# The filter's first layer and its linear part as bfloat16 passes over features split in three stacked parts, from the 61st supertile on, in a graph-convolution kernel

## The chip, the cores and the metric

The kernel runs on one core of a Trainium2 chip. The metric is the device time of one execution in microseconds (us); less is better. Before the change it is 4114.15 us, the median of three runs (4108.7, 4114.15 and 4114.17).

## The reference

A graph layer with N = 12500 nodes, E = 400000 edges sorted by target node (`dst`, the operand that picks rows of h), 128 features and 20 edge attributes:

```python
h = relu(layernorm(x)) @ W_in2f.T                       # 12500 x 128
Wij = smu(f_ij @ W_f1.T + b_f1) @ W_f2.T + b_f2         # the filter, 400000 x 128
x_ij = h[idx_j] * (Wij * rcut_ij[:, None])              # idx_j = dst, sorted
agg = segment_sum(x_ij, idx_i)                          # idx_i = src, in no order
out = x + smu(agg @ W_o1.T + b_o1) @ W_o2.T + b_o2
# smu(z) = ((1 + a) z + (1 - a) z erf(mu (1 - a) z)) / 2, a = 0.01, mu = 2.5
```

`smu` is a scaled GELU plus a small linear part (`LIN`), so the filter is a product with W_f1, a bend, and a product with W_f2. All is float32.

## The kernel before

Edges are handled in tiles of 128, groups of four tiles (512 edges, `GRP`) and supertiles of two groups (1024 edges, `SUP`): 3125 tiles, 782 groups, 391 supertiles. The supertiles are cut into nine epochs (`PARTS`: 59, 59, 59, 59, 48, 37, 27, 27, 16). In an epoch, each tile's 128 messages are scattered into a DRAM buffer with a region for each bin of 128 target rows; in the next epoch that buffer is read back and summed, while the new messages go to the next buffer, and the buffer after that is cleared.

The order on TensorE (PE), VectorE (DVE), ScalarE (ACT) and SyncE (SP) is the order of the code, written by hand; each of these engines works through its queue in that order. One turn of the loop over groups (from L888) does for group g, in software-pipelined order:

- `load(s + 3)` (L431, every second group; SP): the 20 rows of features `f_t` of a supertile (L438) into one of four float32 buffers `fbufs`, whose row 20 holds ones for the bias; then `targets` (L443, the row `rbc` broadcast to 128 partitions, L448) and `window` (L455, two transfers `hw` of 42 rows of h in three bfloat16 parts, L462).
- clearing (L178) of the next buffer, and in `fetch` (L672, L679) reading of the last one, both on SP.
- `turn(g)` (L629): four PE products with w_o1 per group into `pt`; `send(g)` (L638): ACT scales them by the edge weight into `ms` (L642, L645; six buffers of one group each), and GpSimd (POOL) issues four indirect scatters (L648), one per tile.
- `weigh(g + 1)` (L609, L615): the float32 product of w_f2 with the bent layer; `gather` (L596) a bfloat16 one-hot product; `take` (L604) its copy on ACT; `mix` (L620, L625) on DVE.
- `hide(g + 2)` (L555, L562): the float32 product of w_f1 with the features, into `pu`; `bend` (L565, L570): GELU on ACT; `smooth` (L573, L578): `sm = LIN * pu + ge` on DVE, one 128x512 pass.
- `bins`, `count`, `read`, `number`, `pick` (L477 to L551 and L465, L471): places in the buffers, on DVE and PE; `parts`/`add` (L724, L694, L703): the sums of the last epoch's buffer on PE, with `choose` (L690) and the addition to `agg` (L716) on DVE.

In the first epoch, `step` (L877) spreads the setup over the turns: the rows of h (`rows_of_h`, L200 to L230, which split a float32 tile in three bfloat16 parts by `tensor_sub`, L222 and L226) and the index tables. After the last group the last buffer is summed and the output layer is run (L944 to L1022).

Of the kernel before, what the change touches and what calls it, by code (L numbers as in the profile page):

```python
# [19 lines left out]
P = 128  # L20
# [6 lines left out]
LIN = ALPHA / GC  # L27

SUP = 8
GRP = 4  # L30
# [3 lines left out]
ROW = P + 1  # L34
# [6 lines left out]
def gnn_kernel(  # L41
# [19 lines left out]
    nc = tc.nc  # L61
    N, D = x.shape
    R, E = f_t.shape
# [4 lines left out]
    def chunks(total, step):  # L68
        return [(a, min(step, total - a)) for a in range(0, total, step)]
# [28 lines left out]
    const = ctx.enter_context(tc.tile_pool(name="const", bufs=1))  # L98
# [4 lines left out]
    bufs = [dram.tile([NB * CAP[k], ROW], F32, name=f"buf{k}") for k in range(EPOCHS)]  # L103
# [3 lines left out]
    ident = const.tile([P, P], F32, name="ident")  # L107
# [19 lines left out]
    lift = const.tile([P, P], F32, name="lift")  # L127
# [8 lines left out]
    onesb = const.tile([P, P], F32, name="onesb")  # L136
# [2 lines left out]
    NC = (NT + CH - 1) // CH  # L139
    bad = const.tile([P, 4 + 2 * EPOCHS], F32, name="bad")  # L140
    lh = const.tile([P, 2, NC], F32, name="lh")
    b1w = const.tile([P, P], F32, name="b1w")
    nc.vector.memset(bad, 0.0)


# [6 lines left out]
    w_in = const.tile([P, P], F32, name="w_in")  # L152
    w_f1 = const.tile([P, P], F32, name="w_f1")
    w_f2 = const.tile([P, P], F32, name="w_f2")
    b2 = const.tile([P, 1], F32, name="b2")
    b2row = const.tile([1, P], F32, name="b2row")
    b1 = const.tile([P, 1], F32, name="b1")
    bz = const.tile([P, 1], F32, name="bz")
    w_o1 = const.tile([P, P], F32, name="w_o1")
    w_o2 = const.tile([P, P], F32, name="w_o2")  # L160
# [113 lines left out]
    with tc.tile_pool(name="ld", bufs=4) as ld, \  # L274
# [8 lines left out]
        irow_ps = ps1.tile([P, GRP * P], F32, name="irow_ps")[:, 0:P]  # L283
        nc.vector.tensor_copy(irow_ps, irow)

        NF = 4
        fbufs = [ld.tile([P, SUP * P], F32, name=f"f{i}", bufs=1) for i in range(NF)]

        def fill(i, engine):
            engine.memset(fbufs[i], 1.0)  # L290

        FEW = 6 * SUP

        def parts_tile():
            return edge.tile([P, GRP, 3, D], BF, name="hs")

        early = (eps_of[0][1] + 3) * PER

        def bank(name):
            return ps2.tile([P, GRP, P], F32, name="pg")  # L300
# [105 lines left out]
        zr = edge.tile([P, 3 * D], BF, name="zr", bufs=1)  # L406
        nc.gpsimd.memset(zr, 0.0)
        nc.gpsimd.dma_start(h_dram[NB * P:N + P, :], zr[:N + P - NB * P, :])
        fill(3, nc.gpsimd)
        nc.gpsimd.memset(x_sb[:, NB - 1, :], 0.0)  # L410
        spare = const.tile([P, 2], F32, name="spare")
        nc.scalar.activation(spare[:, 0:1], eps, AF.Sqrt)
# [16 lines left out]
        loaded, onehot, bins_of, slots, hidden, taken = {}, {}, {}, {}, {}, {}  # L429

        def load(s):  # L431
            if s >= NS:
                return
            t0, nt = sups[s]
            e0, n = t0 * P, nt * P
            fb = fbufs[s % NF]
            if s > 0:
                nc.sync.dma_start(fb[0:R, :n], f_t[:, e0:e0 + n])  # L438
            loaded[s] = (fb,)
            if s > 2:  # L440
                targets(s)

        def targets(s):  # L443

            t0, nt = sups[s]
            e0, n = t0 * P, nt * P
            rb = ld.tile([P, SUP * P], BF, name="rbc")
            nc.sync.dma_start(rb[:, :n], rel_dram[:, e0:e0 + n].to_broadcast([P, n]))  # L448
            loaded[s] += (rb,)
            if s < FEW // SUP:  # L450
                loaded[s] += (h_first.rearrange("p b k d -> p (b k d)"),)
            else:
                window(s)
# [99 lines left out]
        units_of = {}  # L553

        def hide(g):  # L555

            if g >= NG:
                return
            n = groups[g][1] * P
            o = g % PER * GRP * P  # L560
            pu = ps1.tile([P, GRP * P], F32, name="pu")
            nc.tensor.matmul(pu[:, :n], w_f1, loaded[g // PER][0][:, o:o + n], start=True, stop=True)  # L562
            units_of[g] = pu

        def bend(g):  # L565
# [7 lines left out]
        def smooth(g):  # L573
            if g >= NG:
                return
            n = groups[g][1] * P
            sm = edge.tile([P, GRP * P], F32, name="sm")
            nc.vector.scalar_tensor_tensor(sm[:, :n], units_of.pop(g)[:, :n], LIN, hidden[g][:, :n],  # L578
                                           op0=ALU.mult, op1=ALU.add)
            hidden[g] = sm  # L580

        rows_of = {}

# [25 lines left out]
        def weigh(g):  # L609

            if g >= NG:
                return
            n = groups[g][1] * P
            pw = ps1.tile([P, GRP * P], F32, name="pw")
            nc.tensor.matmul(pw[:, :n], w_f2, hidden.pop(g)[:, :n], start=True, stop=True)  # L615
            pws[g] = pw

        mixed = {}
# [169 lines left out]
        pb1 = spread_group(1)  # L788
# [28 lines left out]
        def output_bias():  # L817

            nc.vector.tensor_scalar(w_o2, w_o2, GC, None, op0=ALU.mult)
            nc.vector.tensor_scalar(bz, b1, ZS, None, op0=ALU.mult)  # L820
            nc.vector.tensor_scalar(b1w, onesb, b1, LIN, op0=ALU.mult, op1=ALU.mult)
            pb1 = bank("pb1")[:, 0, :]
            nc.tensor.matmul(pb1, b1w, w_o2, start=True, stop=True)
            nc.vector.tensor_add(bo2, bo2, pb1)

        def named(make, names):

# [23 lines left out]
        steps = [one["placed"], loads.pop(0), one["limits"]]  # L851
# [18 lines left out]
        for i in range(0, len(units_of_rows), 2):  # L870
            for pair in zip(*units_of_rows[i:i + 2]):
                steps += pair
        steps.append(output_bias)
        COUNT = len(steps)
        taken_steps = slot = 0

# [11 lines left out]
        for g in range(NG):  # L888
            s = g // PER
            k = epoch[s]  # L890
            g0, ng = eps_of[k][0] * PER, min(eps_of[k][1] * PER, NG - eps_of[k][0] * PER)
            i = g - g0
            if g == (FEW // SUP - 3) * PER:
                assert not opening
            if g % PER == 0:
                load(s + 3)
            if i == 0:
                cleared = 0
            if g < BY:

                while at_first < min(len(cleans) - 1, -(-(g - 5) * (len(cleans) - 1) // (BY - 12))):
                    apart(clear(0, at_first, nc.sync), "filled", "cleared")
                    at_first += 1
            elif k + 1 < EPOCHS:
                past = BY if k == 0 else 0
                upto = min(len(cleans), -(-(i + 1 - past) * len(cleans) // (ng - 4 - past)))
                while cleared < upto:
                    clear(k + 1, cleared, nc.sync)
                    cleared += 1
            if k and i == 0:  # L910
                work = [(b, q) for b in range(NB) for q in range(Q[k - 1])]
                done = 0
            if k and i == 1:
                begin(k - 1)
            if k and i == WAIT - 2:
                choose(k - 1, 0)
            lo = hi = 0
            if k and i >= WAIT:
                upto = len(work) - (LEFT if k == EPOCHS - 1 else 0)
                lo = upto * (i - WAIT) // (ng - WAIT)  # L920
                hi = upto * (i + 1 - WAIT) // (ng - WAIT)
            if g:
                turn(g)
                send(g)
            step()
            number(g + 1)
            weigh(g + 1)
            gather(g + 1)
            take(g + 1)
            parts(k - 1, lo + (hi - lo) // 2)  # L930
            mix(g + 1)
            step()
            hide(g + 2)
            bend(g + 2)
            count(g + 2)
            smooth(g + 2)
            if g % PER == 0:
                pick((g + 4) // PER)
            bins(g + 3)
            read(g + 2)  # L940
            parts(k - 1, hi)
            step()
            assert k == 0 or taken_steps == COUNT
        k = EPOCHS - 1  # L944
# [32 lines left out]

        def between():
            unit, ge = opened.pop(0)
            sm = edge.tile([P, GRP * P], F32, name="sm")  # L980
            nc.gpsimd.tensor_add(sm[:, :width(unit)], part_of(unit), ge[:, :width(unit)])
            smoothed.append((unit, sm))

# [55 lines left out]
    with tc.If(flag > 0):  # L1039
        with tc.tile_pool(name="gl", bufs=1) as gl, tc.tile_pool(name="gps", bufs=1, space=PSUM) as gps:  # L1040
# [9 lines left out]
            fb = gl.tile([R + 1, P], F32, name="gfb")  # L1050
            nc.vector.memset(fb, 1.0)
            with tc.For_i(0, NT, 1) as t:
# [119 lines left out]
```

## Time and profile before

| what | value |
|---|---|
| median of three runs | 4114.15 us |
| the profiled execution | 4108.47 us |
| its span, first to last instruction | 4106.6 us |
| PE / DVE / ACT / POOL busy | 3668.0 / 3445.1 / 1948.2 / 3081.7 us |
| scatters on POOL (L648) | 3125, mean 964 ns |
| `smooth` on DVE (L578) | 782, mean 685 ns |
| moved by DMA | 820.83 MB, mean 200 GB/s |
| granted TensorE clock | 0.978 |

The profile is of one execution. The span is the time between its first and last instruction; the remaining 1.9 us of that execution lie around it. [...] The DMA share is the mean busy share of 16 DMA engines. A matmul of float32 is recorded as two passes, one of bfloat16 as one.

### The profile page before, as it was taken

The numbers are of one execution on the slowest core, as the hardware profiler recorded it, in microseconds if no ns is written. First come the engines' busy times: TensorE is split into PE (matmuls) and PEld (weight loads), VectorE is DVE, ScalarE is ACT, GpSimd is POOL, SyncE is SP. The second block draws the span as 40 slices with busy tenths as digits, with TensorE's granted clock in tenths as the row PEclk, the third lists the DMA queues.
The fourth block names the chain that finished last, engine by engine and source line by source line (L and its number), as shares of the span: only waits on it lengthen the run. The fifth ranks groups of instructions, "written<-read, shape, count | busy, mean of one in ns | idle before, by whom it ended". The sixth has DMA issues, their size and how long they took to land.

```text
span 4106.6 us, 74086 instructions
## 1 busy us (share of the span) xinstructions
PE 3668.0 (89%) x21117; PEld 2553.0 (62%) x21117; DVE 3445.1 (84%) x7657; ACT 1948.2 (47%) x5690; POOL 3081.7 (75%) x3199
## 2 busy tenths in 40 slices
PE   7878887998979998979998979999899989999897
PEld 4445545666656666646666656666677667666677
DVE  8898887888868888868888868888899889988896
ACT  4557764544444444434544434444444444444441
POOL 6777777777777777777777777777777777777775
PEclk9999999999999999999999989999999999999999
DMA  6976656776647676757667747777689699887568
GB/s 188 232 189 179 195 166 198 204 201 197 195 130 220 204 204 186 201 152 206 202 197 198 198 147 204 208 204 212 179 229 223 186 244 242 221 228 217 164 194 250
DMA packets 564246, 820.83 MB, mean 200 GB/s; under 512 B 178033, under 2 KB 378488, under 8 KB 563698
## 3 DMA queue, kind: packets, MB, share of 16 engines
q1 hardware_dynamic: 449760, 601.83, 54.7%
q0 software_dynamic: 100320, 207.40, 15.9%
q10 hardware_dynamic: 13746, 6.80, 0.6%
q8 instruction: 167, 2.74, 0.3%
q14 instruction: 253, 2.07, 0.2%
HBM read 442.34 MB, written 373.37 MB: 199 GB/s over the span
## 4 chain that ended last, share of the span: by engine, by line
PE 38%; DVE 28%; DMA 19%; ACT 6%; issue 5%; POOL 2%; DVEq 0%; SPq 0%; ACTq 0%; POOLq 0%
DMA buf<-ms,ix 17%; PE pt L635 11%; PE pg L703 8%; DVE se L690 8%; PE pw L615 8%; PE pu L562 7%; DVE mt L625 5%; DVE so L496 4%; DVE sm L578 3%; DVE sl L540 3%; ACT ms L645 2%; ACT ge L570 2%; POOL buf L648 2%; PE ph L596 2%; DVE agg L716 1%
## 5 line engine op out<-in xcount | busy, mean ns | idle before, releaser
L648 POOL DMA_INDIRECT buf<-ms,ix x3125 | 3011.3, 964 | 981.5 <-issue 384.1
L645 ACT ACTIVATE ms<-pt,w_sb 128x128 f32<-128x128 f32 x3125 | 889.0, 368 | 1122.7 <-PE pt L635 1115.4
L635 PE MATMUL pt<-w_o,mt 128*128 128x128 f32 x6250 | 883.7, 285 | 386.0 <-DVE mt L625 382.4
L703 PEld LDWEIGHTS pg<-se,rw 128*128 128x128 f32 x8036 | 1052.5, 192 | 246.5 <-issue 209.7
L703 PE MATMUL pg<-se,rw 128*128 128x128 f32 x8036 | 1149.1, 280 | 2.9 <-DVE se L690 2.9
L635 PEld LDWEIGHTS pt<-w_o,mt 128*128 128x128 f32 x6250 | 768.5, 194 | 472.9 <-DVE mt L625 468.9
L496 DVE SCALAR_TENSOR_TENSOR so<-irow_ps,hi_f,so 128x98 f16<-128x98 f32 x3116 | 989.5, 318 | 82.6
L615 PE MATMUL pw<-sm,w_f 128*128 128x512 f32 x1564 | 823.0, 609 | 10.7 <-DVE sm L578 8.8
L562 PE MATMUL pu<-f,w_f 128*128 128x512 f32 x1564 | 807.3, 598 | 0.0
L625 DVE SCALAR_TENSOR_TENSOR mt<-pw,b,hg 128x512 f32<-128x512 f32 x782 | 583.9, 747 | 201.3 <-ACT hg L604 198.0
L570 ACT ACTIVATE ge<-pu 128x512 f32<-128x512 f32 x782 | 468.4, 599 | 533.2 <-PE pu L562 524.6
L578 DVE SCALAR_TENSOR_TENSOR sm<-pu,ge 128x512 f32<-128x512 f32 x782 | 535.8, 685 | 185.6 <-ACT ge L570 179.2
L690 DVE TENSOR_TENSOR se<-irow_ps,rw 128x1536 f32<-128x1536 f32 (+1 forms) x345 | 588.0, 1704 | 114.0 <-DMA rw<-buf 109.1
L604 ACT ACTIVATE hg<-ph 128x512 f32<-128x512 f32 x782 | 468.5, 599 | 59.7 <-PE ph L596 42.9
L540 DVE TENSOR_REDUCE sl<-pc 128x4 f32<-128x392 f32 x782 | 434.7, 556 | 0.0
L642 ACT ACTIVATE ms<-lo_b 128x4 f32<-128x4 bf16 x782 | 160.1, 205 | 339.8 <-DMA buf<-ms,ix 339.4
L596 PE MATMUL ph<-oh,hw 126*128 126x512 bf16 x770 | 297.0, 386 | 0.0
L562 PEld LDWEIGHTS pu<-f,w_f 128*128 128x128 f32 x1564 | 251.9, 195 | 52.2 <-issue 40.9
L510 PE MATMUL pc<-so,tri 128*128 128x392 f16 x782 | 257.8, 330 | 0.4 <-DVE so L496 0.2
L615 PEld LDWEIGHTS pw<-sm,w_f 128*128 128x128 f32 x1564 | 241.3, 195 | 23.6 <-DVE sm L578 20.2
L512 PEld LDWEIGHTS <-rest_h 128*128 128x128 f16 x781 | 76.3, 98 | 263.1 <-issue 263.1
L512 PE MATMUL pc<-so,rest_h 128*128 128x294 f16 x781 | 225.5, 289 | 0.0
(153 smaller groups left out, 1386.9 us busy)
## 6 DMA issues: line engine op xcount, KB each, us to landing
rw<-buf SPq DMA_DIRECT2D x292, 774.0 KB
rbc<-rel_dram SPq DMA_DIRECT2D x389, 256.0 KB
buf<-zero SPq DMA_DIRECT2D x243, 387.0 KB
buf<-ms,ix POOLq DMA_INDIRECT x3125
buf<-zero SPq DMA_DIRECT2D x193, 258.0 KB
rw<-buf SPq DMA_DIRECT2D x49, 645.0 KB
f<-in_f_t SPq DMA_DIRECT2D x390, 80.0 KB
hw<-h_dram SPq DMA_DIRECT2D x770, 31.5 KB
```

The lines of the kernel that those rows point to most:

```text
L496: nc.vector.scalar_tensor_tensor(so[:, j], irow_ps[:, :NB], hi_f[:, t + j:t + j + 1], so[:, j - 1] if j else before, op0=ALU.is_equal, op1 ...
L540: nc.vector.tensor_reduce(sl[:, :n], pc[:, :n], op=ALU.max, axis=AX.X)
L562: nc.tensor.matmul(pu[:, :n], w_f1, loaded[g // PER][0][:, o:o + n], start=True, stop=True)
L570: nc.scalar.activation(ge[:, :n], units_of[g][:, :n], AF.Gelu, scale=ZS)
L578: nc.vector.scalar_tensor_tensor(sm[:, :n], units_of.pop(g)[:, :n], LIN, hidden[g][:, :n], op0=ALU.mult, op1=ALU.add)
L615: nc.tensor.matmul(pw[:, :n], w_f2, hidden.pop(g)[:, :n], start=True, stop=True)
L625: nc.vector.scalar_tensor_tensor(mt[:, :n], pws.pop(g)[:, :n], b2, rows_of.pop(g)[:, :n], op0=ALU.add, op1=ALU.mult)
L635: nc.tensor.matmul(pt[:, j, :], mt[:, j * P:(j + 1) * P], w_o1, start=True, stop=True)
L645: nc.scalar.activation(ms[:, j, 0:P], pt[:, j], AF.Copy, scale=w_sb[:, t + j:t + j + 1])
L648: i = nc.gpsimd.indirect_dma_start(out=bufs[k][:, :], out_offset=bass.IndirectOffsetOnAxis(ap=ix[:, j:j + 1], axis=0), in_=ms[:, j, :], in ...
L690: nc.vector.tensor_tensor(se[:, :m], irow_ps.unsqueeze(1).to_broadcast([P, m, P]), rows_in[c][:, :m, P:P + 1].to_broadcast([P, m, P]), op= ...
L703: nc.tensor.matmul(pgs[0][:, g, :], rows_in[c][:, o, 0:P], sel[c][:, o, :], start=(q == 0), stop=(q == Q[k] - 1))
```

## The change

From supertile 60 on (`PLAIN`), the features of a supertile stand as three bfloat16 parts that add up to the float32 value, stacked in one tile: 60 rows of the first part three times, 40 rows of the second twice, 20 rows of the third, and three rows of ones (123 rows). The weights W_f1 stand in three parts opposite to them (`ws_f`), so that one bfloat16 pass over 123 rows gives the product. The linear part `LIN * (W_f1 f + b) W_f2` is a second bfloat16 pass (`ws_c`) that opens the accumulation of `pw`; `smooth` does nothing there. The features come in chunks of six supertiles (`SEG`): one load into `fx` (120 rows), four ACT copies and four DVE subtractions split them, one of these eight in each turn (`splits`), and three SBUF-to-SBUF transfers per supertile stack them (`load`). Six new steps at the end of the first epoch make the weights. `rbc` has three buffers where it had four, `fbufs` three (each of two halves) where it had four; the output layer's `sm` uses the `ms` buffers.

```diff
+        NF = 3
+        HALVES = 2
+        SEG = P // R
+        PLAIN = eps_of[0][1] + 1
+        fx = ld.tile([P, SUP * P], F32, name="fx", bufs=1)
         def fill(i, engine):
             engine.memset(fbufs[i], 1.0)
+            engine.memset(fbufs[i][96:P, :].bitcast(BF), 1.0)
...
-        fill(3, nc.gpsimd)
...
-            if s > 0:
+            if s >= PLAIN:
+                fb = stack_of(s)
+                c, j = (s - PLAIN) // SEG, (s - PLAIN) % SEG
+                a = 0
+                for q in range(3):
+                    r = 3 - q
+                    nc.sync.dma_start(fb[a:a + r * R, :n],
+                                      parts_of[c][j * R:(j + 1) * R, q, :n].unsqueeze(1).to_broadcast([R, r, n]))
+                    a += r * R
+            elif s > 0:
                 nc.sync.dma_start(fb[0:R, :n], f_t[:, e0:e0 + n])
...
+        def split(c, i):
...
+            if i < 0:
+                if whole:
+                    nc.sync.dma_start(fx[0:whole * R, :],
+                                      f_t[:, e0:e0 + whole * SUP * P].rearrange("k (s e) -> s k e", e=SUP * P))
...
+            part = parts_of[c]
+            kind, half = i // 2, i % 2
+            o = half * (SUP * P // 2)
...
+            f32, of = fx[:rows, o:o + w], lambda q: part[:rows, q, o:o + w]
+            if kind == 0:
+                nc.scalar.activation(of(0), f32, AF.Copy)
+            elif kind == 1:
+                nc.vector.tensor_sub(f32, f32, of(0))
+            elif kind == 2:
+                nc.scalar.activation(of(1), f32, AF.Copy)
+            else:
+                nc.vector.tensor_sub(of(2), f32, of(1))
+        def splits(g):
+            c, i = divmod(g - PER * (PLAIN - 3 - SEG) - 4, PER * SEG)
+            if c >= 0 and i < 8:
+                split(c, i)
+            if c >= -1 and i == 8:
+                split(c + 1, -1)
...
-            rb = ld.tile([P, SUP * P], BF, name="rbc")
+            rb = ld.tile([P, SUP * P], BF, name="rbc", bufs=3)
...
-            nc.tensor.matmul(pu[:, :n], w_f1, loaded[g // PER][0][:, o:o + n], start=True, stop=True)
+            w = w_f1 if g // PER < PLAIN else ws_f
+            nc.tensor.matmul(pu[:, :n], w, loaded[g // PER][0][:, o:o + n], start=True, stop=True)
...
-            sm = edge.tile([P, GRP * P], F32, name="sm")
-            nc.vector.scalar_tensor_tensor(sm[:, :n], units_of.pop(g)[:, :n], LIN, hidden[g][:, :n],
-                                           op0=ALU.mult, op1=ALU.add)
-            hidden[g] = sm
+            pu, ge = units_of.pop(g), hidden[g]
+            if g // PER < PLAIN:
+                nc.vector.scalar_tensor_tensor(ge[:, :n], pu[:, :n], LIN, ge[:, :n], op0=ALU.mult, op1=ALU.add)
...
-            nc.tensor.matmul(pw[:, :n], w_f2, hidden.pop(g)[:, :n], start=True, stop=True)
+            folded = g // PER >= PLAIN
+            if folded:
+                nc.tensor.matmul(pw[:, :n], ws_c, loaded[g // PER][0][:, o:o + n], start=True, stop=False)
+            nc.tensor.matmul(pw[:, :n], w_f2, hidden.pop(g)[:, :n], start=not folded, stop=True)
...
+        def crossed():
+            nc.gpsimd.memset(ws_f, 0.0)
+            nc.gpsimd.memset(ws_c, 0.0)
...
+        weight_steps = [crossed, combined, lambda: cut_weights(w_f1, pieces()[0]), lambda: cut_weights(lift, pieces()[1]),
+                        stacked, restored]
...
             smooth(g + 2)
+            splits(g)
...
-            sm = edge.tile([P, GRP * P], F32, name="sm")
+            sm = msg.tile([P, GRP, ROW], F32, name="ms").rearrange("p b r -> p (b r)")[:, :GRP * P]
```

More of the change, by code (lines that the diff above doesn't have):

```diff
@@ L141, in gnn_kernel @@
     lh = const.tile([P, 2, NC], F32, name="lh")
-    b1w = const.tile([P, P], F32, name="b1w")
     nc.vector.memset(bad, 0.0)
@@ L154, in gnn_kernel @@
     w_f2 = const.tile([P, P], F32, name="w_f2")
+    ws_f = const.tile([P, P], BF, name="ws_f")
+    ws_c = const.tile([P, P], BF, name="ws_c")
     b2 = const.tile([P, 1], F32, name="b2")
@@ L284, in gnn_kernel, with stack_of @@
         nc.vector.tensor_copy(irow_ps, irow)
-        NF = 4
+        NF = 3
+        HALVES = 2
+        SEG = P // R
+        assert SEG >= 6 and 6 * R + 3 <= P
+        PLAIN = eps_of[0][1] + 1
         fbufs = [ld.tile([P, SUP * P], F32, name=f"f{i}", bufs=1) for i in range(NF)]
+        fx = ld.tile([P, SUP * P], F32, name="fx", bufs=1)
         def fill(i, engine):
             engine.memset(fbufs[i], 1.0)
+            engine.memset(fbufs[i][96:P, :].bitcast(BF), 1.0)
+        def stack_of(s):
+            half = s // NF % HALVES
+            return fbufs[s % NF].bitcast(BF)[:, half * SUP * P:(half + 1) * SUP * P]
         FEW = 6 * SUP
         def parts_tile():
-            return edge.tile([P, GRP, 3, D], BF, name="hs")
+            whole = edge.tile([P, 3, SUP * P], BF, name="hs").rearrange("p q e -> p (q e)")
+            return whole[:, :GRP * 3 * D].rearrange("p (n k d) -> p n k d", k=3, d=D)
         early = (eps_of[0][1] + 3) * PER
@@ L441, in load, with chunk_of @@
                 targets(s)
+        parts_of = {}
+        def chunk_of(c):
+            s0 = PLAIN + c * SEG
+            return s0, min(SEG, NS - s0)
+        def split(c, i):
+            s0, m = chunk_of(c)
+            if m <= 0:
+                return
+            e0, whole = sups[s0][0] * P, sum(sups[s0 + j][1] == SUP for j in range(m))
+            rows = m * R
+            cols = sups[s0][1] * P if m == 1 else SUP * P
+            if i < 0:
+                if whole:
+                    nc.sync.dma_start(fx[0:whole * R, :],
+                                      f_t[:, e0:e0 + whole * SUP * P].rearrange("k (s e) -> s k e", e=SUP * P))
+                for j in range(whole, m):
+                    n = sups[s0 + j][1] * P
+                    e = sups[s0 + j][0] * P
+                    nc.sync.dma_start(fx[j * R:(j + 1) * R, :n], f_t[:, e:e + n])
+                return
+            if i == 0:
+                parts_of[c] = edge.tile([P, 3, SUP * P], BF, name="hs")
+            part = parts_of[c]
+            kind, half = i // 2, i % 2
+            o = half * (SUP * P // 2)
+            w = min(cols, o + SUP * P // 2) - o
+            if w <= 0:
+                return
+            f32, of = fx[:rows, o:o + w], lambda q: part[:rows, q, o:o + w]
[13 more added lines that the diff above has]
+                split(c + 1, -1)
         def targets(s):
@@ L614, in weigh @@
             pw = ps1.tile([P, GRP * P], F32, name="pw")
-            nc.tensor.matmul(pw[:, :n], w_f2, hidden.pop(g)[:, :n], start=True, stop=True)
+            o = g % PER * GRP * P
+            folded = g // PER >= PLAIN
+            if folded:
+                nc.tensor.matmul(pw[:, :n], ws_c, loaded[g // PER][0][:, o:o + n], start=True, stop=False)
+            nc.tensor.matmul(pw[:, :n], w_f2, hidden.pop(g)[:, :n], start=not folded, stop=True)
             pws[g] = pw
@@ L820, in output_bias, with pieces, combined, cut_weights @@
             nc.vector.tensor_scalar(bz, b1, ZS, None, op0=ALU.mult)
-            nc.vector.tensor_scalar(b1w, onesb, b1, LIN, op0=ALU.mult, op1=ALU.mult)
+            nc.vector.tensor_scalar(lift, onesb, b1, LIN, op0=ALU.mult, op1=ALU.mult)
             pb1 = bank("pb1")[:, 0, :]
-            nc.tensor.matmul(pb1, b1w, w_o2, start=True, stop=True)
+            nc.tensor.matmul(pb1, lift, w_o2, start=True, stop=True)
             nc.vector.tensor_add(bo2, bo2, pb1)
+        kept = [None]
+        def pieces():
+            return kept[0][:, :, 0:P], kept[0][:, :, P:2 * P]
+        def crossed():
+            nc.gpsimd.memset(ws_f, 0.0)
+            nc.gpsimd.memset(ws_c, 0.0)
+            kept[0] = edge.tile([P, 3, SUP * P], BF, name="hs")
+            pb = bank("pb1")[:, 0, :]
+            nc.tensor.transpose(pb, w_f1, ident)
+            nc.scalar.activation(lift, pb, AF.Copy)
+        def combined():
+            pb = bank("pb1")[:, 0, :]
+            nc.tensor.matmul(pb, lift, w_f2, start=True, stop=True)
+            nc.vector.tensor_scalar(lift, pb, LIN, None, op0=ALU.mult)
+        def cut_weights(w, to):
+            nc.scalar.activation(to[:, 0], w, AF.Copy)
+            nc.vector.tensor_sub(onesb, w, to[:, 0])
+            nc.scalar.activation(to[:, 1], onesb, AF.Copy)
+            nc.vector.tensor_sub(to[:, 2], onesb, to[:, 1])
+        def stacked():
+            for w, to in zip((ws_f, ws_c), pieces()):
+                a = 0
+                for q in range(3):
+                    r = 3 - q
+                    nc.sync.dma_start(w[a:a + r * R, :], to[0:R, 0:r, :])
+                    a += r * R
+                for q in range(3):
+                    nc.sync.dma_start(w[a + q:a + q + 1, :], to[R:R + 1, q, :])
+        def restored():
+            nc.vector.memset(onesb, 1.0)
+        weight_steps = [crossed, combined, lambda: cut_weights(w_f1, pieces()[0]), lambda: cut_weights(lift, pieces()[1]),
+                        stacked, restored]
         def named(make, names):
@@ L873, in gnn_kernel @@
         steps.append(output_bias)
+        steps += weight_steps
         COUNT = len(steps)
```

## The prediction, made before the changed kernel was run

> **What bounds the kernel now.** First the page's busy times, its chain of waits and its costliest group:
>
> ```profile
> PE 3668.0 (89%) x21117; PEld 2553.0 (62%) x21117; DVE 3445.1 (84%) x7657; ACT 1948.2 (47%) x5690; POOL 3081.7 (75%) x3199
> ...
> PE 38%; DVE 28%; DMA 19%; ACT 6%; issue 5%; POOL 2%; DVEq 0%; SPq 0%; ACTq 0%; POOLq 0%
> ...
> L648 POOL DMA_INDIRECT buf<-ms,ix x3125 | 3011.3, 964 | 981.5 <-issue 384.1
> ```
>
> These name PE and DVE, the engines that the change relieves. The third line speaks against them: POOL's 3125 scatters last 964 ns and have 981.5 us of idle before them, 0.31 us each. Is that waiting, or the price of issuing a scatter? The busy times in equal stretches of 500 us tell (columns: PE, PEld, DVE, ACT, POOL, clock, DMA share, GB/s; then one of 220 us):
>
> ```profile
> 2000.00:2500.00 500.00, 441.24 (x2533) 306.81 (x2531) 406.96 (x890) 227.35 (x675) 379.60 (x395) 0.98 0.66 188
> 3000.00:3500.00 500.00, 479.35 (x2931) 349.10 (x2930) 442.49 (x937) 231.59 (x684) 378.19 (x395) 0.99 0.88 225
> 3300.00:3520.00 220.00, 216.10 (x1345) 159.14 (x1344) 200.86 (x412) 100.88 (x299) 165.78 (x173) 1.00 0.96 240
> ```
>
> PE's work differs by 38 us between the first two, yet POOL issues 395 scatters in both: 1.266 us each. POOL's timeline, start to start, shows the same step with the same 0.30 us of idle, whatever is named as its releaser. So POOL never pauses: the first scatter starts at 19.9 us, the last ends at 4002.5, and 3125 steps of 1.264 us are 3950 of these 3983 us. The chain passes POOL by because it follows each 0.30 us to whichever instruction ended last before it. Of real waiting (idle over 0.33 us, less the 0.30) I count 17.6 us before 640 us, 3.5 from there to 3870, and 7.7 to 4002, where PE is 137 of 140 us busy. After 4002 come 104 us of last sums and outputs. **POOL sets the pace**, 4 x 1.266 = 5.06 us per group; a change pays only where POOL waits, and costs wherever POOL is held.
>
> **PE and DVE.** 662 of 782 groups change (391 - 60 = 331 supertiles). On PE, a float32 product of 512 columns takes 0.86 us start to start (L615 to L596 at 2007.41), a bfloat16 one 0.22 (L596 to L703): hide falls by 0.64, weigh grows by 0.22, 0.42 x 662 = 278 us less. On DVE, 662 x 0.685 = 453 us of smooth go; 224 subtractions (56 chunks x 4) come at 0.683 (L226, 128x512), 153 us. ACT gains 224 copies at 0.644 (L225), 144 us, beside its 47% busy. As POOL has the pace, what all this can save is the waiting in the turns from 640 us on, 3.5 + 7.7 = 11.2 us: bounds -11.2 and 0; I take **-8**, nearly all of it in the last epoch, where one group less 0.42 us of PE fits again into 5.06 us.
>
> **POOL held by the subtractions.** Elongated scatters tell what holds POOL. Scatters, then DVE, near 405 us:
>
> ```profile
> 403.90 0.96 POOL L648 DMA_INDIRECT buf<-ms,ix  x1 [0.30 <-issue]
> 405.16 1.36 POOL L648 DMA_INDIRECT buf<-ms,ix  x1 [0.31 <-DVE mt L625]
> 406.83 0.95 POOL L648 DMA_INDIRECT buf<-ms,ix  x1 [0.30 <-ACT ms L645]
> 408.08 1.47 POOL L648 DMA_INDIRECT buf<-ms,ix  x1 [0.30 <-DVE sl L540]
> ```
>
> ```profile
> 405.00 0.68 DVE L226 TENSOR_TENSOR hs<-rw,hs 128x512 bf16<-128x512 f32 x1
> 408.03 0.69 DVE L226 TENSOR_TENSOR hs<-rw,hs 128x512 bf16<-128x512 f32 x1
> ```
>
> Where L226 runs at a scatter's start, that scatter ends some 0.27 us after L226 plus its own length: 0.40 and 0.51 us late. L226 subtracts one SBUF tile from another; L222, the same size with one operand in PSUM, touches 27 scatters and lengthens none, L226 touches 28 and lengthens 10, by 2.76 us in all, 0.106 us for each of its 26. The 224 new subtractions are of L226's form (fx and hs in SBUF, 120x512). So 224 x 0.106 = **+24 us**, straight on POOL's path. Bounds: 0, if none lies on a start (the loop keeps DVE and POOL in step, so phases come in runs, as those of L471 do), and 224 x 0.51 = +114. I take the mean of the 26.
>
> [...]
>
> **Transfers.** A supertile's features came as 20 packets of 4 KB (about 0.20 us each in the trace's packet records, 4.0 us of one engine). They still come so, through fx, and 120 packets of 2 KB are added for the stack. rbc's 2 KB packets took 0.121 us: 14.5 us, over 16 engines 0.91 us per supertile of 10.1, or +9 points of DMA share from 640 us on. Where the share is 0.66 nothing is late. At 3300 to 3520 it is 0.96 already, and 1.05 does not fit: the highest of 50 us was 0.98, so some 7% of 220 us, 15 us, are short. In 2930 to 3250 0.87 + 0.09 just fits. The cover is `ms`: five groups ahead are 25 us of POOL's work. [...] I take **+15**.
>
> Edits at nothing: SP issues two more transfers per supertile (L438 0.39 us each) where it waits 52 of 220 us for PE even in the busiest stretch; the stacks' wait for the subtraction lies one turn behind it, and what stands behind it on SP (rbc, hw, fetch) is needed two turns later. fx is needed four turns (20 us) after its issue; late, it would hold ACT and, through it, `ms`. Two memsets on POOL (0.19 us each, L392) add 0.5 us. The first fill's extra DVE memset lies ahead of the 5.1 us that the CAST at L304 waits anyway. The output's sm shares six `ms` buffers, two per unit, three units deep: 0, ±2.
>
> **Sum.** The profiled execution took 4108.5 us (span 4106.6 and 1.9 around it): 4108.5 - 8 + 24 + 15 + 0.5 = 4140. It stands near the lowest of the runs shown; their median is 5.7 above it. I add half of that: **4143 us**.
>
> **Rivals.**
> 1. *The DMA engines become the bound* from 2930 to 3800. The share is a mean over 16 engines, but f's 20 packets never ran more than 11 at once and the 252 of two hw transfers never more than six, so some engines carry f, hw and now most of the stack. [...] For it: SP's transfers took 8 to 10 us from issue to last packet near 3410. [...]
>    [...]
> 2. *The subtractions hold nothing* and `ms` covers the transfers: 4143 - 24 - 15 = 4104, or 4119 with the transfers late. For it: 18 of 28 touched scatters kept their length.
> 3. *Faster, by PE's relief in the last epoch*: place 3870 to 4002, price 11 us at most, 4143 - 24 - 15 - 3 = 4101; it decides if subtractions and transfers together cost under 3 us. Were the chain of waits right, the 278 us of PE would pass through: 3830; the constant 395 scatters exclude it but for a few per cent.
> 4. *The passes do not do what they say* (no shorter on PE): only the 8 us are lost, within the forecast's range.
>
> **How the numbers follow.** About 0.2%, 8 us, is what a measurement of this kernel can tell from no change; around 4114 that is 4106 to 4122. Forecast 0.50 (4122 to 4175), rival 1 0.22 (4175 to 4230), rival 2 0.17 (4106 to 4122), rival 3 0.11 (below 4106). So slower 0.72, same 0.17, faster 0.11. The range 4100 to 4205 leaves out some 0.06 below and 0.10 above. The forecast's own is 4122 to 4175.
>
> **What would show it.** POOL's step outside the subtractions stays 1.26 us; scatters that start in a subtraction are 0.1 to 0.5 us longer, in sum about 24 us more than now; smooth's 662 instructions gone, hide one pass of 0.22 us; DMA share up by 9 points from 640 us on; waits of POOL, if any, at 3300 to 3520. It is wrong if scatters at subtractions keep 0.96 us, if POOL's step itself shortens, or if POOL waits before 2900 us.

## The result, and the profile after

The changed kernel takes **4158.51 us** (median of four runs, 4157.05 to 4159.44); the kernel before took 4113.42 beside it (four runs). The ratio is 1.0112, with a 95% interval of 1.0099 to 1.0126: slower by 1.1%, 15 us above the forecast of 4143 and inside its own range (4122 to 4175). The profiled execution of after took 4159.27 us, its span is 4157.1, its granted clock 0.951.

The page of after, the three lines that answer to those of before:

```profile
PE 3475.2 (84%) x20793; PEld 2591.2 (62%) x21120; DVE 3170.3 (76%) x7226; ACT 2088.5 (50%) x5919; POOL 3109.5 (75%) x3202
...
DMA 32%; PE 30%; DVE 20%; ACT 7%; issue 5%; POOL 2%; SPq 2%; ACTq 0%; DVEq 0%; POOLq 0%
...
L721 POOL DMA_INDIRECT buf<-ms,ix x3125 | 3036.0, 972 | 1005.4 <-issue 372.0
```

PE has 193 us less to do and DVE 275, and the kernel is 50 us longer: neither was the bound. POOL's 3125 scatters have grown from 964 to 972 ns, and the idle time before them by 24 us. These two numbers are the loss: 8 ns x 3125 = 25 us, and 24. The stretches show where (columns as before):

```profile
2000.00:2500.00 500.00, 404.93 (x2449) 307.37 (x2495) 360.75 (x818) 243.04 (x701) 380.74 (x392) 0.95 0.73 211
3000.00:3500.00 500.00, 438.43 (x2781) 344.55 (x2826) 389.56 (x842) 246.52 (x694) 373.69 (x385) 0.95 0.86 241
3300.00:3520.00 220.00, 187.91 (x1188) 147.24 (x1205) 168.86 (x357) 103.25 (x294) 160.81 (x166) 0.94 0.86 241
```

From 2000 to 2500 us POOL issues 392 scatters where it issued 395, but is busier for it (380.74 against 379.60): it is held, not waiting. From 3000 to 3500 it issues 385 and is less busy (373.69 against 378.19): it waits. So there are two losses at two places. Split by the records of POOL (too long: what a scatter takes over 0.958 us, where over 0.975; waits: idle before it over 0.33 us, less the 0.30 of its issue):

| kernel | first scatter | scatters too long | waits before 640 | 640 to 3250 | 3250 to 3880 | after 3880 | last scatter's end to span's end |
|---|---|---|---|---|---|---|---|
| before | 19.90 | 18.4 | 7.6 | 0.7 | 2.8 | 7.7 | 104.1 |
| after | 22.87 | 43.4 | 11.3 | 1.1 | 22.6 | 8.1 | 102.8 |
| difference | +3.0 | +25.0 | +3.7 | +0.4 | +19.8 | +0.4 | -1.3 |

The sum is +51.0; the spans differ by 50.5. (The prediction's 17.6 us of waits before 640 us include the 10.0 before the first scatter, which stand in the first column here.)

The first column is not the same in each execution. Seven profiles have the head of after: their first scatter starts at 22.87 us (after and 2), at 21.7 to 21.9 (3, 6 and 7) and at 20.78 and 20.79 (1 and 5). Of the +3.0, 0.9 is in all of them; the rest comes and goes. Before has one profile.

**The holds.** Scatters of after near 2160 us, then the subtractions of the split on DVE:

```profile
2159.24 0.95 POOL L721 DMA_INDIRECT buf<-ms,ix  x1 [0.30 <-ACT ms L718]
2160.49 1.41 POOL L721 DMA_INDIRECT buf<-ms,ix  x1 [0.30 <-ACT ge L640]
...
2165.99 1.21 POOL L721 DMA_INDIRECT buf<-ms,ix  x1 [0.30 <-issue]
```

```profile
2160.39 0.68 DVE L498 TENSOR_TENSOR fx<-fx,hs 120x512 f32<-120x512 f32 x1
2165.68 0.68 DVE L498 TENSOR_TENSOR fx<-fx,hs 120x512 f32<-120x512 f32 x1
```

The two scatters that start inside a subtraction end 0.83 us after it does (2160.39 + 0.68 + 0.83 = 2161.90). That is the median of the clearly held ones, for L498 and for L502. So a scatter that starts in a subtraction does nearly nothing until it is over, and then takes 0.83 of its 0.958 us: the delay is what is left of the subtraction, less 0.13 us. Of 129 scatters that start inside one of the 224 subtractions, 105 are longer, by 27.0 us in all. For a start at any moment of 0.682 us the mean of that delay is 0.55 x 0.55 / 2 / 0.682 = 0.22 us, and 129 x 0.22 = 29.

The order decides. In 175 other scatters a subtraction begins after the scatter's start, and all of them keep 0.95 to 0.96 us; a scatter, then a subtraction that begins 0.28 us into it:

```profile
2103.17 0.96 POOL L721 DMA_INDIRECT buf<-ms,ix  x1 [0.30 <-issue]
```

```profile
2103.45 0.68 DVE L498 TENSOR_TENSOR fx<-fx,hs 120x512 f32<-120x512 f32 x1
```

So it is a scatter's start that is held, not all of its work.

**The waits.** What POOL and DVE waited for from 3250 to 3880 us (in total, times, longest), after and then before:

```profile
POOL buf L721 <- ACT ms L718: 49.1, 93, 4.0
...
DVE oh L540 <- DMA rbc<-rel_dram: 31.1, 12, 5.0
DVE se L763 <- DMA rw<-buf: 26.3, 7, 10.6
```

```profile
POOL buf L648 <- ACT ms L645: 29.6, 97, 0.3
...
DVE se L690 <- DMA rw<-buf: 18.1, 2, 11.7
```

Before, POOL's 97 idle times behind `ms` are 0.3 us each: its own issue, no wait. After, 93 of them hold 49.1 us, up to 4.0 each, so 49 - 93 x 0.30 = 21 us are real. Behind that stands a new line: DVE's one-hot `oh` waits 31.1 us for `rbc`, a transfer that SP issues right behind the stack's three.

### The profile page after: what moved, and what is told of

Its sections match the earlier page's. It is cut to its first block, busy times and chain, and to the rows that moved or that the text cites. A ratio compares the mean times of both kernels' runs of the same rounds, so it can differ in the third digit from the quotient of the medians.

```text
span 4157.1 us, 74955 instructions
## 1 busy us (share of the span) xinstructions
PE 3475.2 (84%) x20793; PEld 2591.2 (62%) x21120; DVE 3170.3 (76%) x7226; ACT 2088.5 (50%) x5919; POOL 3109.5 (75%) x3202
## 4 chain that ended last, share of the span: by engine, by line
DMA 32%; PE 30%; DVE 20%; ACT 7%; issue 5%; POOL 2%; SPq 2%; ACTq 0%; DVEq 0%; POOLq 0%
DMA buf<-ms,ix 24%; PE pt L708 10%; PE pw L688 8%; PE pg L776 6%; DVE se L763 5%; DVE mt L698 5%; DMA rw<-buf 3%; DMA rbc<-rel_dram 3%; ACT ms L718 3%; DVE so L565 2%; ACT hg L673 2%; POOL buf L721 2%; PE ph L665 2%; DVE sl L609 2%; PE pu L632 1%
## 5 line engine op out<-in xcount | busy, mean ns | idle before, releaser
L708 PE MATMUL pt<-w_o,mt 128*128 128x128 f32 x6250 | 918.4, 292 | 577.5 <-DVE mt L698 574.7
L776 PEld LDWEIGHTS pg<-se,rw 128*128 128x128 f32 x8036 | 1065.4, 194 | 262.5 <-issue 224.0
L708 PEld LDWEIGHTS pt<-w_o,mt 128*128 128x128 f32 x6250 | 793.1, 199 | 675.0 <-DVE mt L698 670.5
L688 PE MATMUL pw<-ge,w_f 128*128 128x512 f32 x1564 | 858.3, 632 | 32.9 <-DVE ge L649 11.4
L688 PEld LDWEIGHTS pw<-ge,w_f 128*128 128x128 f32 x1564 | 304.9, 201 | 57.4 <-DVE ge L649 23.0
L632 PE MATMUL pu<-f,ws_f 128*128 128x512 bf16 x659 | 252.6, 383 | 0.0
L540 DVE TENSOR_SCALAR oh<-rbc,prow 128x1024 bf16<-128x1024 bf16 x385 | 191.7, 498 | 50.8 <-DMA rbc<-rel_dram 50.6
L665 PEld LDWEIGHTS <-hw 126*128 126x128 bf16 x770 | 78.5, 102 | 201.7 <-issue 170.8
L789 DVE TENSOR_TENSOR agg<-agg,pg 128x512 f32<-128x512 f32 (+1 forms) x200 | 134.2, 671 | 81.3 <-PE pg L776 79.1
```

The costliest lines, as they stand in the source:

```text
L665: nc.tensor.matmul(ph[:, :n], hw[:3 * WIN, g % PER, :], oh[:3 * WIN, o:o + n], start=True, stop=True)
L708: nc.tensor.matmul(pt[:, j, :], mt[:, j * P:(j + 1) * P], w_o1, start=True, stop=True)
L776: nc.tensor.matmul(pgs[0][:, g, :], rows_in[c][:, o, 0:P], sel[c][:, o, :], start=(q == 0), stop=(q == Q[k] - 1))
```

## The experiments

Each is an edit of the changed kernel. The kernel before ran beside each: 4115.92 us for the first four, 4111.02 for the next three, 4111.33 for the last two. Ratios are to it, with 95% intervals; "after" stands for 1.0112.

**1. One operand of each subtraction in PSUM.** Same size, same place; it subtracts a ramp and not the first part, so the parts are other numbers.

```
-                nc.vector.tensor_sub(f32, f32, of(0))
+                nc.vector.tensor_sub(grid(f32), grid(f32), ramp)    # ramp: irow_ps, in PSUM
...
-                nc.vector.tensor_sub(of(2), f32, of(1))
+                nc.vector.tensor_sub(grid(of(2)), grid(f32), ramp)
```

> The changed kernel, but each of its 224 subtractions takes the index ramp that lies in PSUM as second operand, where it took the bfloat16 part in SBUF; place, size, output and first operand stay, so the parts that are summed are not those of the features. Theory (a subtraction of two SBUF tiles holds POOL at a scatter's start): the scatters' length above 0.958 us, 27.0 us inside the subtractions in the trace of the changed kernel, falls to under 3 us, and the time by some 25 us, from 4158 to about 4133. Rival (the subtractions cost by being there, as DVE work or through their output): the same 27 us and 4158.

4140.60 us, 1.0066 (1.0048 to 1.0084). A subtraction on DVE, then the scatter that starts in it:

```profile
2154.39 0.68 DVE L500 TENSOR_TENSOR fx<-fx,irow_ps 120x512 f32<-120x512 f32 x1
```

```profile
2154.70 0.96 POOL L723 DMA_INDIRECT buf<-ms,ix  x1 [0.30 <-issue]
```

The subtraction is as long as in after, and the scatter that starts inside it keeps 0.96 us. 119 scatters start in one, ten are longer, by 0.7 us in all instead of 27.0; all scatters together are 18.2 us too long, as before the change (18.4). That settles the holds, and what makes them: the second operand in SBUF. The time fell by 18 us and not by 25, since the waits from 3250 to 3880 us rose from 22.6 to 31.3. That fits a POOL that is held less and asks for its messages earlier while the transfers come no earlier; in 12, which has no stack either, these waits are gone.

**2. No stacking transfers from the second chunk on** (products see old stacks; copies, subtractions, `fx` and passes stay).

```
-                for q in range(3):
+                for q in range(3 if c == 0 else 0):
```

> The changed kernel without the three stacking transfers from the seventh changed supertile on: the first six stacks are used again and again, so the filter is that of other edges there. Splits and loads of fx stay. Theory (added transfers make POOL wait from 3250 to 3880 us): the DMA share falls by about 9 points, POOL's waits of 22.5 us in that stretch fall to under 5, and the time to about 4138; the 27 us of the subtractions stay. Rival (these waits come from SP or DVE order, or from the subtractions' own delay): waits stay above 15 us, time above 4150.

4133.54 us, 1.0047 (1.0029 to 1.0065). From 3250 to 3880 us:

```profile
DVE se L763 <- DMA rw<-buf: 52.6, 3, 19.9
POOL buf L721 <- ACT ms L718: 29.9, 98, 0.3
```

`rbc` is gone from the list, POOL's idle times are 0.3 us again, and its waits from 3250 us on fall from 30.7 to 1.8. DVE still waits for `rw`, twice as long, and POOL doesn't notice: not each long wait in that list is a loss.

**3. The passes alone**: as 2, and no `fx`, copies and subtractions from the second chunk on either.

```
+            if m <= 0 or c > 0:    # in split
```

> The changed kernel without splits, loads of fx and stacking transfers from the second chunk on: the first six stacks are used again, so the filter is that of other edges there. What is left of the change are the bfloat16 passes, the smooth that is gone, and fewer transfers than before. Theory (POOL's 3125 scatters set the pace, PE's and DVE's relief is worth only POOL's waits): 4105, between 4098 and 4113. Rival (the chain of waits is right, PE and DVE have the pace): some 280 us less, about 3830.

4108.39 us, 0.9982 (0.9972 to 0.9992). All of the passes' relief and none of their costs but the head's is worth 0.2%, 7.5 us: the chain of waits, by which PE and DVE were two thirds of the time, is refuted as a guide here.

**4. The bfloat16 fill at the end of the first epoch** instead of in the head: the line goes from `fill`, three memsets on DVE come into `restored`.

> The changed kernel, but the three bfloat16 fills of the stacks' last rows (1.76 to 1.80 us each) move from the head to the last of the weight steps, on DVE, where POOL is not held. Theory (the fill in DVE's head order delays the first index cast, and with it the first scatter, from 19.9 to 22.9 us): the first scatter starts at about 20 us and the time falls by 3 us or a little more, to about 4155. Rival (the head's three us come from elsewhere, such as the granted clock): first scatter at 22 us or later, 4158.

4152.19 us, 1.0093 (1.0075 to 1.0111); the first scatter at 18.48 us. The gain is 6.3 us (0.19%, or 8 us, by the ratios, whose intervals overlap); the first scatter is 4.4 us earlier than in the profile of after, and 2.3 earlier than in those of 1 and 5. The waits before 640 us were 5.8 instead of 11.3. In the kernels here that keep the fill in the head they lie between 7.2 and 11.3, in two others without it (11 and 12) at 8.9 and 9.5, so how much of this is the fill's isn't shown.

**5. The same bytes in the same number of 2 KB packets, by other blocks**: blocks of 48, 64 and 8 rows per supertile and not 60, 40 and 20 (each row from its own part, so the stacks hold other rows).

```
...
+                    for q, (a, b) in enumerate([(0, 48), (48, 112), (112, 120)]):
+                        nc.sync.dma_start(fb[a:b, :n], parts_of[c][a:b, q, :n])
...
```

> The changed kernel, but a stack's 120 rows come from the split tile by blocks of 48, 64 and 8 rows, which 16 divides or 8, where they came as 60, 40 and 20: three transfers and 120 packets of 2 KB as before, of other rows, so the filter is that of other features. Theory of rival 1 (some DMA engines carry f, hw and the stack, and these are the bound): spread over 16 engines the packets fit; POOL's waits from 3250 us on fall from 30.7 us to under 12, the time to about 4140. Rival (the sum of the packets counts, however spread): waits above 22 us, 4158 within 5.

4138.02 us, 1.0065 (1.0048 to 1.0081). From 3250 to 3880 us:

```profile
POOL buf L725 <- ACT ms L722: 33.5, 97, 2.5
...
DVE oh L544 <- DMA rbc<-rel_dram: 18.8, 7, 5.2
```

POOL's waits from 3250 us on are 9.4 instead of 30.7. These 21 us are 73% of the 29 that no stack at all takes away (2), so most of the transfers' cost hangs on how the three transfers are made up: which rows, and how many in each. The queue's packets took 59.9% of 16 engines' span where they took 60.0%, so they did not become shorter by other rows being read. Whether they lie on other engines isn't shown: the trace's records name none.

**6. The stack issued behind `rbc` and `hw`** instead of ahead of them.

```
+            loaded[s] = (fb,)
+            if s > 2:
+                targets(s)
             if s >= PLAIN:
...
-            loaded[s] = (fb,)
-            if s > 2:
-                targets(s)
```

> The changed kernel, with the three stacking transfers issued behind rbc and hw of the same supertile, where they were ahead of them; nothing is left out. DVE waited 50.6 us for rbc in the changed kernel, whose transfer is due two turns after its issue, the stack's four. Theory (rbc behind the stack's packets is what comes late): DVE's waits for rbc fall below 20 us, POOL's waits from 3250 us on by some 10 us, the time to about 4148. Rival (the engines are full, the order only moves the wait to another transfer): 4158 within 5, with waits for rw in place of those for rbc.

4141.87 us, 1.0069 (1.0053 to 1.0086): 17 us for the order of three issues. The waits from 3250 us on are 13.6 instead of 30.7, those of `oh` for `rbc` over the whole run 25.1 instead of 50.6. The prediction had argued that `rbc` is needed two turns later and so is not hurt by what is queued ahead; it is. What 5 and 6 gain is not added up: no run here has both.

**7. The stack's three transfers with 64 of 1024 columns** from the second chunk on: as many instructions, rows and packets, a sixteenth of the bytes.

```
-                    r = 3 - q
+                    r, w = 3 - q, n if c == 0 else 64
...
```

> [...] Theory (the bytes that the engines carry make POOL wait): waits from 3250 us on under 6 us, the time near that without these transfers, 4133.5, at most 4138. Rival (the number of transfers counts: SP's issues, or eight in flight at most): waits stay above 20 us, 4150 or more.

4128.39 us, 1.0038 (1.0024 to 1.0052), the waits from 3250 us on 1.2 us. At least as good as no stack: bytes cost, and neither the number of packets nor SP's issuing.

**8 to 10. Causes together.** Three kernels ran on one chip that took 5036.06 us for the kernel before.

> The late bfloat16 fill (alone 6.3 us) and the stack issued behind rbc and hw (alone 16.6 us) in one kernel. Theory: two separate causes, at two ends of the run, so the gains add: 4158.5 - 6.3 - 16.6 = 4136 us, the first scatter at 18.5 us as with the fill alone, POOL's waits from 3250 us on about 14 us, scatters still about 43 us too long in sum. Rival: what the first scatter gains is waited out again in a later stage, since the loop is bound by transfers there: 4142 us, with waits of POOL some 6 us higher.

> Like the kernel with the late fill and the later stack, and the split itself done with one operand of each subtraction in PSUM: ACT copies a piece of 384 columns to PSUM as well, DVE subtracts the first part from it there, and the second part from what is left. The whole of the reference is computed. Theory: the 224 holds go (25 us), and as with the PSUM operand alone POOL's waits rise by some 8 us where transfers are short: 4136 - 25 + 8 = 4119 us, scatters in sum 18 us too long as before the change. Rival: ACT's three more copies per chunk and the waits of ACT and DVE for each other inside a turn make ms late: POOL waits before 3250 us too, 4130 us or more.

> The late fill, the PSUM operand that stands for the second part (it subtracts other numbers), and no stacking transfers from the second chunk on (its products see old stacks): all three costs out, the copies, subtractions, fx and the passes in. Theory: the three terms are all that the change costs, and the passes themselves bring nothing: 4158.5 - 25 (holds) - 25 (stack) - 6 (fill) = 4102, or 4105 by the passes alone (4108.4) with the better head. Rival: ACT's 224 copies or fx cost something of their own: 4115 us or more. Rival: with everything out the relief of PE shows: below 4095 us.

5165.95 us (1.0263; 1.0239 to 1.0287), 5212.27 (1.0360; 1.0327 to 1.0392) and 4992.61 (0.9920; 0.9895 to 0.9946). The group of scatters in the first of them:

```profile
L719 POOL DMA_INDIRECT buf<-ms,ix x3125 | 3028.1, 969 | 2008.9 <-ACT ms L716 1176.7
```

POOL's instructions are no longer than elsewhere, but its idle time has doubled to 2009 us: here the loop waits for `ms`, since PE, DVE and ACT pause for microseconds between instructions (ACT starts L716 at 2005.19 us, 5.06 after its last work and 3.6 after the product that it reads). DMA packets last as long as in the kernel of 6 (a mean of 77 ns against 80 on SP's queue), so it isn't slow packets. The granted clock was 0.89 (0.96 in 6); whether that is cause or effect isn't shown, and what it is stays open. Where POOL doesn't set the pace the terms can't be told from the time, so the second and the third ran once more elsewhere (11 and 12). The first did not: whether the gains of 4 and 6 add by themselves can't be told.

**11. The whole of the reference, with three mends**: the late fill of 4, the order of 6, and the split done in PSUM, in pieces of 384 columns beside `irow_ps` in its bank.

```
+                nc.scalar.activation(of(0), f32, AF.Copy)
+                nc.scalar.activation(res, f32, AF.Copy)      # res: in PSUM
...
+                nc.vector.tensor_sub(res, res, of(0))
+                nc.scalar.activation(of(1), res, AF.Copy)
...
+                nc.vector.tensor_sub(of(2), res, of(1))
```

> The kernel with the late fill, the later stack and the split with a PSUM operand once more, since the chip of its first run took 5036 us for the kernel before, with PE, DVE and ACT pausing for microseconds between instructions in every stage. If the kernel before is back at 4110 to 4116 us here: theory, 4119 us (holds gone, 25 us less; waits of POOL some 8 us more than with the late fill and the later stack; 18 us of scatters too long, as before the change). Rival: ACT's three more copies per chunk, and ACT and DVE waiting for each other inside a turn, make ms late, so that POOL waits before 3250 us too: 4130 us or more.

4117.51 us, 1.0014 (1.0004 to 1.0024). Scatters are 17.7 us too long in sum, as before the change; the waits are 8.9, 0.4, 15.2 and 4.2 in the four stretches, so ACT's added copies cost nothing up to 3250 us. Of the 1.12% that the change cost, 0.14% are left (6 us), and the waits from 3250 to 3880 us, 15.2 against 2.8 before, are the largest part.

**12. All three costs out**: 1, 2 and 4 in one kernel.

> The kernel with all three costs out once more, for the same reason. If the kernel before is back at 4110 to 4116 us here: theory, the holds (25 us), the stack (25 us) and the fill (6 us) are all that the change costs, and the passes themselves bring nothing: 4102 to 4108 us. Rival: ACT's 224 copies or fx cost something of their own: 4115 us or more. Rival: with everything out the relief of PE shows: below 4095 us.

4101.96 us, 0.9976 (0.9966 to 0.9985). From 3250 to 3880 us:

```profile
POOL buf L722 <- ACT ms L719: 28.4, 93, 0.3
```

This kernel is 1.0112 - 0.9976, or 56 us, below after. The three terms make 56 as well, if the holds go in with the 25 us that POOL's records give, beside 25 of stack and 6.3 of fill; by the time alone, 1 gained 18, so one by one they make 49, and the other 7 or so are the waits that 1 added and that need the stack. To within some 6 us, which the two intervals leave, nothing else in the change costs. Against before 9 us are gained in the medians, but 4.0 in the spans of the two profiles: 1.4 by the first scatter and 6.5 by POOL's waits from 640 us on (4.7 against 11.2), less 4 in the waits before 640, the scatters and the tail. The rest of the 9 is in no profile. So the passes bring a little after all.

## Why the prediction held, step by step

The forecast was 29 us above before, and 45 were measured. By the profiles the terms were to make 31.5 and made 51: 8.8 of the difference are the waits that were to go, 4.8 the transfers, 1 the holds, and 4.9 head and tail. All four missed the same way, and the range was wide enough for that.

*What bounds the kernel: right.* POOL's step of 1.264 us decided. With the costs out, all the relief of PE and DVE was worth 7.5 us (3) and 9.4 (12).

*-8 for the waits that PE's relief saves: it did not come.* POOL's waits after 3880 us stayed at 8.1 (7.7 before), though PE was busy for 121 of 140 us there. The mechanism is real: without the stack's bytes (2, 3, 7 and 12) these waits are 0 to 1.8 us. With them, POOL comes into the last epoch out of waits that last up to it (7.7 us from 3700 to 3880), probably without messages ahead, so that the relief goes into catching up; that reading was not tested by itself. This is the term of the sum that failed, and it was a term for a loop whose transfers are on time, put beside one that says they are not.

*+24 for the holds: right, 27.0 measured.* The mean of 26 rows, 0.106 us, became 0.121 over 224. The lower bound, that the phases come in runs and none is hit, did not come. A term of 0, as in the second rival, is refuted: 27.0 us with two operands in SBUF, 0.7 with one in PSUM (1). Only scatters that start inside a subtraction are held (105 of 129, against none of the 175 in which one begins later); how the subtraction does it, no run here shows.

*+15 for the transfers: mechanism right, size and place too small.* 19.8 us of waits in 3250 to 3880, and by 2 and 7 some 25 to 30 us of time. Of the 22.6 us of after, 8.9 lie in 3300 to 3520, where all were forecast, and 13.4 behind it. The term was worked out from the mean DMA share, 1.05 that doesn't fit into 1. That share was 0.96 at 3300 to 3520 before and is 0.86 now, while transfers are late: a mean over 16 engines was not the limit. (At 2000 to 2500 us it rose by 7 points, where 9 were forecast.) How the stack's transfers are made up was worth 21 us of the waits (5), and their order on SP 17 (6), which the prediction had put at nothing.

*0 for the head: +3.0 in these profiles.* The step that was named held: DVE's fill (1.76 us) was hidden by the CAST. DVE after, then POOL after, then DVE before:

```profile
3.95 1.76 DVE L297 MEMSET f<- 32x2048 bf16 x1 [0.48 <-DVE rest_h L133]
...
10.07 0.74 DVE L822 TENSOR_SCALAR oh<-pg,pcol 128x512 bf16<-128x512 f32 x1
10.74 1.21 DVE L847 TENSOR_SCALAR w_f<-w_f 128x128 f32<-128x128 f32 x1
```

```profile
10.06 1.80 POOL L297 MEMSET f<- 32x2048 bf16 x1
```

```profile
10.11 0.75 DVE L749 TENSOR_SCALAR oh<-pg,pcol 128x512 bf16<-128x512 f32 x1
10.77 0.22 DVE L774 TENSOR_SCALAR w_f<-w_f 128x128 f32<-128x128 f32 x1
```

At 10.07 us DVE is on time. What was missed are the same fills on POOL: while one runs (10.06 to 11.86), the scaling of `w_f` on DVE takes 1.21 us instead of 0.22, and DVE is 0.9 late from there. PE then pauses 1.11 us where it paused 0.20, and in this execution its next products run at about half the rate for longer. PE after, then before:

```profile
17.27 1.91 PE L688 MATMUL pw<-ge,w_f 128*128 128x512 f32 x2
...
20.10 2.08 PE L708 MATMUL pt<-w_o,mt 128*128 128x128 f32 x8 [0.92 <-DVE mt L698]
```

```profile
16.00 1.13 PE L615 MATMUL pw<-sm,w_f 128*128 128x512 f32 x2
...
18.05 1.16 PE L635 MATMUL pt<-w_o,mt 128*128 128x128 f32 x8 [0.92 <-DVE mt L625]
```

0.9 + 0.8 + 0.9, and 0.5 in the gathers between, are the 3 us. Only the first 0.9 is shown to be the fill's: 1 and 5 have the same pause at 15.39 us, then `pw` at 16.89 in 1.12 and 1.13 us, and their first scatter at 20.8. The two added memsets of the prediction's +0.5 run on POOL at 12.54 and 12.69 us, ahead of the first scatter. The tail, put at 0 with 2 either way, came 1.3 us shorter. Before 640 us POOL waited 3.7 us more. The prediction had named waits before 2900 us as a sign against it; kernels here with the same code up to there differ by as much (7.2 to 11.3).

*The rivals.* 1, the DMA engines as the bound: other blocks of rows took 21 us of the waits away (5), but which engines were full is not shown, and its range (4175 to 4230) was not reached; the transfers cost 25 to 30. 2, no holds: refuted. 3, faster by PE: refuted as 3830, and as 4101 true only of kernels without the costs (12). 4: `hide` is one pass (L632, bfloat16, 383 ns each, 0.22 from its start to the next product's), and 193 us of PE's time are gone, so the passes do what they say. Of the 278 us that were worked out, `hide` gave what it should, 425 (0.64 x 662); `weigh` took 172 more where 146 were worked out (the trace keeps 341 of the 662 records of its new pass, so both the 172 and the 193 may be somewhat off), and the products of `turn`, which the change leaves alone, took 35 more (292 ns each instead of 285).

The terms were -8 + 24 + 15 + 0.5 + 0, and came as +0.8 (waits from 640 to 3250 us and after 3880), +25.0, +19.8, and 3.0 + 3.7 - 1.3 in head and tail.

## What to carry to other kernels

Find the engine whose step is constant, and price a change by what it holds and starves that engine: hundreds of microseconds of DVE and PE bought 9 at most, and 224 small subtractions cost 27 us, since a scatter that started under one had to wait for its end; one operand in PSUM took that away. Transfers that were added where the mean DMA share stood at 0.96 cost 25 to 30 us, by their bytes (7), by how they were made up (5) and by what they were queued ahead of (6), so look at row counts and at the order of issue before the mean share. A gain that needs slack elsewhere must not be added to a sum whose other terms take that slack.

## What the runs showed of the hardware that was not expected

A scatter on POOL that starts under a DVE subtraction of two SBUF tiles isn't slowed by a share but stopped until that ends (105 of 129 longer; end to end 0.83 us, median of L498 and L502 alike). One that has started when the subtraction begins keeps its length (175 of 175, 0.95 to 0.96 us).

The hold also works the other way: a POOL memset of 1.80 us kept a DVE tensor_scalar of 0.22 us for 1.21. How either comes about isn't shown.

PE's products ran at about half the rate at first: `pw` 1.91 us at 17.27 after, 1.13 at 16.00 before. The pause of 1.11 us at 15.39 is not enough for it: 1 and 5 have it too, with `pw` in 1.12 and 1.13 us. What halved the rate isn't shown: the profile's clock reads 1.00 from 11 to 25 us in after and in before.

The mean granted clock is 0.951 where it was 0.978, and 0.94 to 0.95 in stretches that had 0.98 to 1.00, with PE less busy in each. What lowers it isn't shown; the longer products of `turn` may be that.
